# Value products after every step of a 16-dim attention: a kept bank for the sums, three banks in rotation for the scores

## The chip, the cores and the metric

The kernel runs on one core of a Trainium2 chip. A core has TensorE (PE; matrix products, with weight loads on PEld), VectorE (DVE), ScalarE (ACT), GpSimd (POOL) and SyncE (SP), which run side by side and wait for each other by semaphores. TensorE writes only to PSUM, which here is handed out in banks of 128 partitions by 512 fp32 numbers; eight of them exist. VectorE and ScalarE read the banks. The metric is the device time of one execution in microseconds (us); lower is better.

## The reference

Two transformer layers over 1024 tokens of width 256, in fp32, each with an attention and a mixture of experts. The first layer's attention is a gated sum of two: a main one with 16 heads of 192 dims, and a "pattern" attention with 16 heads of 16 dims. The change concerns the second:

```python
pq = split_heads(hidden_states @ sp_q_w.T)
pk = split_heads(hidden_states @ sp_k_w.T)
pv = split_heads(hidden_states @ sp_v_w.T)
p_scores = jnp.einsum('bhqd,bhkd->bhqk', pq, pk) * PD ** (-0.5)
p_probs = jax.nn.softmax(p_scores.astype(jnp.float32), axis=-1).astype(dt)
p_ctx = jnp.einsum('bhqk,bhkd->bhqd', p_probs, pv)
pattern_out = p_ctx.transpose(0, 2, 1, 3).reshape(b, s, HID) @ sp_o_w.T
```

All 1024 keys are seen by every query (no mask). The second layer's attention has 16 heads of 16 dims too, with a causal mask and a bias per head; it runs through the same functions with `causal=True`.

## The kernel before

**Banks.** PSUM is one pool. Two tiles named `sc` take two banks each (`sc_tile`, L52). The other four banks are single: two named `nn` and two named `mm`. `mm_tile` (L55) hands them out in turn, nn, mm, nn, mm, so that a bank comes back after four tiles; a tile that is handed out waits until the last reader of the tile before it in that bank is done.

**The 16-dim attention** (`small_attention`, L253). Four heads form a group; each head sits in 32 of the 128 partitions, so that four score products with 32 rows each run side by side in the four row groups of the array. A unit is one half of the queries (512) and one group of heads: eight units. The work has two sides:

- First scores (`first_pair`, L286): queries on the partitions, 512 keys along the free dimension, two heads into one `sc` tile (L299). VectorE takes the maximum per query (L305, `mx`). When all maxima of a unit are there, `find_maximum` and `put_maximum` turn them over on TensorE (L319, a single bank) and VectorE adds them to the queries (L323, `q2`), so that the second scores come out with the maximum taken off.
- Second scores (`second_pair`, L326): keys on the partitions, 512 queries along the free dimension (L337). ScalarE takes the exponential out of PSUM into `pt`, of one head from a single bank (L347), or, where a step is `wide`, of two heads from an `sc` tile (L344).

A step is one unit and one block of 128 keys: 8 x 8 = 64 steps. As long as first scores of later units are left (steps 0 to 52), a step puts two of them (L299, one `sc` tile each) beside its four second scores: `together(first_pair(*now[0], pair), second(1 - pair))` for two values of `pair`, so two groups of four products. From step 53 on no first scores are left; then odd steps are wide, and even steps put their four second scores into four single banks.

**Value products** (`over_v`, L360). `pt` is multiplied with the values of its key block (L369), four heads into four column groups of one bank `av`. Every second step, in step i with i odd, the products of steps i-3 and i-2 are added up in one single bank from the rotation, eight products in a block. Then ScalarE copies the bank into `cu` where the steps are the unit's first (L375), or VectorE adds it to `cu` (L377). Two steps after the unit's last sum, `divided` (L380) turns `cu` over on TensorE (L385, a single bank), and VectorE divides by the sums of the exponentials.

**Order.** In this stage the order on TensorE is the order in which the program writes it (`tc.manual_schedule` for PE); the other engines' instructions are put in order by the scheduling layer. The stage is driven by the loop of `n_steps` steps with a few products of other work beside steps 38, 39, 53, 55, 57 and 59 (`beside`): the output product of the first half and parts of the main attention's first keys and queries (L655, L668). After it come the main attention's scores (`score_products`, L701, L708).

**Elsewhere** `mm_tile` serves every other product of one bank: projections, transposes, the main attention's four sums (L957), the experts. In the last experts the pool is split: `singles[:] = ["mm", "mm"]`, and the two sums of `modulated_experts` hold the two `nn` banks, then the two `mm` banks.

Of the kernel before, what the change touches and what calls it, by code (L numbers as in the profile page):

```python
# [8 lines left out]
F32 = mybir.dt.float32  # L9
# [5 lines left out]
P = 128  # L15
# [27 lines left out]
def adaln_two_layers(ctx: ExitStack, tc: tile.TileContext, a: dict, out: bass.AP):  # L43
# [5 lines left out]
    psum = ctx.enter_context(pool("psum", 2, space=bass.MemoryType.PSUM))  # L49


    sc_tile = lambda: psum.tile([P, T], F32, tag="sc", name="sc")  # L52
    singles = ["nn", "mm"]

    def mm_tile(tag=None):  # L55
        if tag is None:
            tag = singles[0]
            singles.reverse()
        return psum.tile([P, 512], F32, tag=tag, name=tag)

    turn = [0]

# [114 lines left out]
    def whole(parts):  # L177
        for _ in parts:
            pass
# [73 lines left out]
    def small_attention(sp, qT, kT, v, causal, late):  # L253
# [103 lines left out]
            for it in pairs:  # L357
                next(it, None)

        def over_v(some):  # L360

            u, kc0 = steps[some[0]][:2]
            half, g = units[u]
            av = mm_tile()
            for n in some:
                _, kc, _, q0, _ = steps[n]
                pt = probs.pop(n)
                for j in range(4):
                    nc.tensor.matmul(  # L369
                        av[PW * j : PW * (j + 1), q0:], v[:, kc, 4 * g + j, :], pt[:, j, q0:],  # L370
                        start=(n == some[0]), stop=(n == some[-1]),
                    )
            if kc0 == 0:
                state[u]["cu"] = late[0].tile([P, 512], F32, name="cu", bufs=2)
                nc.scalar.copy(state[u]["cu"], av)  # L375
            else:
                nc.vector.tensor_add(state[u]["cu"], state[u]["cu"], av)  # L377
            return u if steps[some[-1]][2] else None
# [16 lines left out]
        steps = []  # L395
# [26 lines left out]
        ends = []  # L422

        def step(i):
            if i < len(steps):
                u, kc, last, q0, nkc = steps[i]
                probs[i] = late[0].tile([P, 4, 512], F32, name="pt", bufs=6)
                now = [it for _, it in zip(range(counts[i]), beside)]
                for it in now[1:]:
                    first(*it)  # L430


                wide = not now and (causal or i % 2 == 1)
                second = lambda pair: second_pair(u, kc, pair, probs[i], q0, wide)
                if now:
                    for pair in range(2):
                        together(first_pair(*now[0], pair), second(1 - pair))
                else:
                    together(second(0), second(1))
            if i % 4 == 3 and causal and ends:  # L440
                divided(ends.pop())
            go = 4 if causal else 2
            if i % go == 1 and i > go:
                ended = over_v(range(i - go - 1, i - 1))
                if ends:
                    divided(ends.pop())
                if ended is not None:
                    ends.append(ended)
            if i % 4 == 1:
                if i < len(steps) and kc == nkc - 3 and u + 1 < len(units):  # L450
                    find_maximum(u + 1)
                    put_maximum(u + 1)
# [34 lines left out]
    with pool("l0a") as l0, pool("mla") as ml:  # L487
# [228 lines left out]
        with pool("pat") as pat:  # L716
# [142 lines left out]
            with pool("pat2") as pat2:  # L859
                nrm = pat2.tile([P, 4, NH, 16], F32, name="nrm")  # L860

                nrms = [nrm, acc[1].rearrange("p t (h d) -> p t h d", d=16)]
                late += [pat2, nrms]
                mp[0] = pat2

                def put(i, t, ps):
                    nc.vector.tensor_scalar_mul(acc[i][:, t, :], ps, gsm[:, 4 * i + t, 1:2])

                output = small_output(
                    in_two(acc[1].rearrange("p (k i) d -> p k (i d)", k=2)), nrm, sp_o, put, 0
                )
                beside = {
                    38: [lambda: next(output)],
                    39: [lambda: whole(output)],
                    53: [lambda: whole(key_part(0, 0, True))],
                    55: [lambda: whole(query_part(0, 0, True, True))],
                    57: [lambda: whole(key_part(0, 1, True))],
                    59: [lambda: whole(query_part(0, 0, False, True))],  # L880
                }
                with tc.manual_schedule(engines={mybir.EngineType.PE}):
                    for n in range(n_steps):
                        step(n)
                        for fn in beside.get(n, []):
                            fn()
                    score_products(0)
                    last_divided()
                    score_products(1)

        with pool("mla1") as m1, pool("mla2", 2) as m2:
            mp[0] = m2
# [10 lines left out]
            prs, sums, pts, cxs, bcs, rws, avs = {}, {}, {}, {}, {}, {}, {}  # L903
# [93 lines left out]
            for u, (p, i) in enumerate(units):  # L997
                n = 8 * u
# [299 lines left out]
        gate_rows[i] = gD  # L1298
        yield

    def modulated_experts(i, tag, bank):


        sums = [mm_tile(tag) for _ in range(2)]
        chunks = {}

        def hidden(c):
            w = load(a["moe_w"][c].rearrange("p (b m) -> p b m", b=2))
            w1 = w[:, 0, :].rearrange("p (k m) -> p k m", k=2)
            if c % 2 == 0:  # L1310
                chunks["he"] = he_tile()
            ps, he = bank[0](), chunks["he"][:, c % 2, :]
            for k in range(2):
                nc.tensor.matmul(ps, w1[:, k, :], hT[i][:, k, :], start=(k == 0), stop=(k == 1))  # L1314
            nc.scalar.activation(he, ps, AF.Relu, bias=b1[:, c : c + 1])  # L1315
            rows = [(n, r0, r1) for n, r0, r1 in OWNED if r0 < (c + 1) * P and r1 > c * P]
            if len(rows) > 1 or rows[0][0] != NE1:
                g = row_tile()
                for n, r0, r1 in rows:
                    p0, p1 = max(r0 - c * P, 0), min(r1 - c * P, P)  # L1320
                    by = gate_rows[i][n, :].partition_broadcast(p1 - p0) if n is not None else gate_rows[i][:NE1, :]
                    nc.sync.dma_start(g[p0:p1, :], by)
                nc.vector.tensor_mul(he, he, g)  # L1323
            chunks[c] = (he, w[:, 1, :])

        def down(c, b):
            he, w2 = chunks[c]
            for t in (2 * b, 2 * b + 1):

                nc.tensor.matmul(  # L1330
                    sums[b][:, t % 2 * HID : (t % 2 + 1) * HID], he[:, t * P : (t + 1) * P], w2,
                    start=(c == 0 and t % 2 == 0), stop=(c == NC1 - 1 and t % 2 == 1),
                )

        for c in range(NC1):
            hidden(c)
            yield
            if c > 1:
                for b in range(2):
                    down(c - 2, b)  # L1340
                del chunks[c - 2]
                yield

        ov = out.rearrange("o (t p) d -> p (o t) d", p=P)
        for b in range(2):
            for c in (NC1 - 2, NC1 - 1):
                down(c, b)
            yield
            for t in (2 * b, 2 * b + 1):
                at = tmp.tile([P, HID], F32, name="at")  # L1350
                nc.vector.tensor_mul(at, sums[b][:, t % 2 * HID : (t % 2 + 1) * HID], gates_bc[1][:, HID:])
                nc.vector.tensor_add(x[i][:, t, :], x[i][:, t, :], at)
            nc.sync.dma_start(ov[:, 4 * i + 2 * b : 4 * i + 2 * b + 2, :], x[i][:, 2 * b : 2 * b + 2, :])
# [24 lines left out]
    with tc.manual_schedule(engines={mybir.EngineType.PE}):  # L1378
# [49 lines left out]
        bank, half = [mm_tile], [None]  # L1428

        def beside_experts(n):  # L1430
            step(n)
            do(n)
            if n == 37:
                singles[:] = ["mm", "mm"]
                half[0] = modulated_experts(0, "nn", bank)
            if n >= 38:
                next(half[0])

# [6 lines left out]
    with tc.manual_schedule(engines={mybir.EngineType.PE}):  # L1445
        last_divided()
        bank[0] = lambda: sc_tile()[:, :512]
        output = small_output(in_two(he_tile()), nrm, wo, put, 1, bv, (ones, bo))
        inputs = experts_input(1, nc.vector)
        do = side({  # L1450
            1: [(output, 1)], 3: [(output, 2), (inputs, 5)], 9: [(inputs, 1)], 11: [(inputs, 6)], 18: [(inputs, 2)],
        })
        for n, _ in enumerate(half[0]):
            do(n)
        whole(modulated_experts(1, "mm", bank))

# [125 lines left out]
```

## Time and profile before

| quantity | us |
|---|---|
| median of three runs | 1316.52 |
| lowest and highest of them | 1314.94, 1316.79 |
| span of the profiled execution | 1313.1 |
| TensorE busy | 1279.2 |
| VectorE busy | 831.3 |
| ScalarE busy | 625.2 |
| first scores, L299 in this stage, from and to | 75.8 to 256.2 |
| value products of this stage, L369, from and to | 85.3 to 295.3 |

The page gives no time of the profiled execution but its span; the three runs lie 1.8 to 3.7 us above that span. A line of the timeline reads: start, length (us), engine, source line, operation, output <- inputs, shapes, how often (like instructions that overlap or follow each other are merged), and in brackets how long the engine stood before it and what ended the wait. An fp32 product shows as two passes on TensorE, so one product counts as two MATMUL records. A line of the table of stretches reads: the stretch, its length, and for each engine busy us (and instructions), then the granted TensorE clock, the DMA share and GB/s. The granted clock is 1.00 in all stretches.

### The profile page before, as it was taken

Reading aid. Unit: us, or ns where it says so; the run is one execution under the profiler, and the core shown is the slowest. Engines: PE = TensorE matmul, PEld = TensorE weight load, DVE = VectorE, ACT = ScalarE, POOL = GpSimd, SP = SyncE. Lnnn points to the kernel's source line nnn. Section 1 sums busy time; section 2 is a strip of 40 time slices with the busy share of each in tenths; the row PEclk is TensorE's granted clock in tenths of the full one; section 3 lists DMA queues with packets and bytes.
Section 4 is the critical chain, followed back from the end, with each engine's and each line's share of the span. In section 5 each row is a group of like instructions: output and inputs, shape, how many; then the busy total and the mean of one; then the engine's idle time right before and its main releaser. Section 6 shows DMA issues by size and latency. Waiting matters only on the chain.

```text
span 1313.1 us, 25185 instructions
## 1 busy us (share of the span) xinstructions
PE 1279.2 (97%) x10588; PEld 691.4 (53%) x10588; DVE 831.3 (63%) x1282; ACT 625.2 (48%) x1161; POOL 244.3 (19%) x241
## 2 busy tenths in 40 slices
PE   9999999999999999999999999999989999999998
PEld 6532233334555555555555566655656554566665
DVE  4678887737787787888778875344556675252222
ACT  5366665665756657575665433121055565312121
POOL 5000000042535345253533010000000040020000
PEclk9999999999999999999999999999999999999999
DMA  9200000000000000000005022222210000435441
GB/s 281 57 0 1 1 1 1 1 1 17 10 5 6 6 5 6 6 9 2 2 1 162 2 58 70 80 79 70 69 44 10 1 2 9 107 94 164 147 151 56
DMA packets 56666, 58.82 MB, mean 45 GB/s; under 512 B 15143, under 2 KB 42280, under 8 KB 56554
## 3 DMA queue, kind: packets, MB, share of 16 engines
q1 hardware_dynamic: 56010, 57.22, 14.8%
q8 instruction: 83, 1.36, 0.5%
q14 instruction: 29, 0.24, 0.1%
q10 hardware_dynamic: 544, 0.00, 0.0%
HBM read 55.05 MB, written 1.12 MB: 43 GB/s over the span
## 4 chain that ended last, share of the span: by engine, by line
PE 90%; DVE 7%; issue 1%; ACT 1%; DMA 0%; POOL 0%; DVEq 0%; ACTq 0%; POOLq 0%
PE sc L708 16%; PE sc L299 11%; PE mm L957 6%; PE sc L1314 6%; DVE mx L305 4%; PE sc L1198 4%; PE nn L369 4%; PE mm L369 3%; PE nn L1330 3%; PE nn L957 3%; PE mm L1330 3%; PE nn L1176 2%; PE nn L1198 2%; PE mm L1176 2%; PE mm L1198 2%; PE nn L668 2%
## 5 line engine op out<-in xcount | busy, mean ns | idle before, releaser
L305 DVE TENSOR_REDUCE mx<-sc 128x2 f32<-128x1024 f32 (+3 forms) x224 | 239.6, 1106 | 58.2 <-PE sc L299 15.6
L299 PE MATMUL sc<-kT,qT 32*128 32x512 f32 (+3 forms) x896 | 205.0, 584 | 18.4 <-DVE mx L305 18.0
L916 ACT ACTIVATE pr<-sc,nmax 128x1024 f32<-128x1024 f32 x128 | 142.5, 1113 | 166.1 <-DVE nmax L712 160.2
L337 PE MATMUL nn<-q,kT 32*128 32x512 f32 (+3 forms) x384 | 188.0, 589 | 0.0
L337 PE MATMUL mm<-q,kT 32*128 32x512 f32 (+3 forms) x384 | 186.8, 592 | 0.5 <-DVE qf L673 0.5
L925 DVE STREAM_TRANSPOSE pt<-pr 128x1024 f32<-128x1024 f32 x128 | 157.2, 1236 | 40.9 <-ACT pr L916 40.7
L712 DVE TENSOR_REDUCE nmax<-sc 128x1 f32<-128x1024 f32 x128 | 154.2, 1215 | 42.1 <-PE sc L708 40.2
L347 ACT ACTIVATE pt<-nn 128x512 f32<-128x512 f32 (+1 forms) x192 | 106.9, 557 | 59.4 <-PE mm L337 42.8
L347 ACT ACTIVATE pt<-mm 128x512 f32<-128x512 f32 (+1 forms) x192 | 106.9, 557 | 53.7 <-PE nn L337 22.6
L708 PE MATMUL sc<-kf,qf 128*128 128x512 f32 x256 | 120.7, 604 | 2.2 <-ACT pr L916 2.0
L708 PE MATMUL sc<-x,qf 128*128 128x512 f32 x256 | 121.0, 604 | 1.2 <-ACT pr L916 1.1
L957 PE MATMUL mm<-pt,kv 32*64 32x256 f32 x2048 | 122.0, 378 | 0.0
L957 PE MATMUL nn<-pt,kv 32*64 32x256 f32 x2048 | 120.2, 378 | 0.7 <-ACT bc L944 0.7
L299 PEld LDWEIGHTS sc<-kT,qT 32*128 32x128 f32 x896 | 66.3, 183 | 102.0 <-DVE mx L305 86.6
L1323 DVE TENSOR_TENSOR he<-he,row 128x512 f32<-128x512 f32 x46 | 31.7, 692 | 128.9 <-ACT he L1315 100.9
L637 POOL TENSOR_TENSOR t<-t,cos 128x512 f32<-128x512 f32 x32 | 40.7, 1272 | 348.6 <-PE sc L337 217.4
L957 PEld LDWEIGHTS mm<-pt,kv 32*64 32x64 f32 x2048 | 83.5, 131 | 21.9 <-issue 6.2
L957 PEld LDWEIGHTS nn<-pt,kv 32*64 32x64 f32 x2048 | 86.7, 131 | 15.1 <-DVE acc L980 5.3
L1315 ACT ACTIVATE he<-sc,b 128x512 f32<-128x512 f32 x43 | 29.5, 687 | 123.3 <-PE sc L1314 123.3
L1314 PE MATMUL sc<-hT,w 128*128 128x512 f32 x172 | 80.7, 593 | 0.0
L708 PEld LDWEIGHTS sc<-kf,qf 128*128 128x128 f32 x256 | 45.6, 189 | 57.8 <-issue 54.1
L708 PEld LDWEIGHTS sc<-x,qf 128*128 128x128 f32 x256 | 45.6, 190 | 57.7 <-issue 51.4
(378 smaller groups left out, 2116.5 us busy)
## 6 DMA issues: line engine op xcount, KB each, us to landing
w<-in_moe_w_dram SPq DMA_DIRECT2D x50, 256.0 KB
w<-in_wg_dram SPq DMA_DIRECT2D x16, 256.0 KB
w<-in_wu_dram SPq DMA_DIRECT2D x16, 256.0 KB
w<-in_wd_dram SPq DMA_DIRECT2D x16, 256.0 KB
row<-gD SPq DMA_DIRECT2D x14, 256.0 KB
x<-in_x_dram SPq DMA_DIRECT2D x4, 512.0 KB
wo<-in_o_dram SPq DMA_DIRECT2D x1, 2048.0 KB
wm<-in_wmod_dram SPq DMA_DIRECT2D x6, 256.0 KB
```

What stands on the lines that cost most here:

```text
L299: nc.tensor.matmul(sc[:, i, :n], qT[r, g, qt * P : (qt + 1) * P], kT[r, g, c * 512 : c * 512 + n], start=True, stop=not diag,)
L305: nc.vector.tensor_reduce(mx[:, qi, c, 2 * pair : 2 * pair + 2], sc[:, :, :n], AX.X, ALU.max)
L337: nc.tensor.matmul(ps[:, q0:], kT[r, g, kc * P : (kc + 1) * P], state[u]["q2"][r, q0:], start=True, stop=not diag,)
L347: nc.scalar.activation(pt[:, 2 * pair + i, q0:], ps[:, q0:], AF.Exp)
L369: nc.tensor.matmul(av[PW * j : PW * (j + 1), q0:], v[:, kc, 4 * g + j, :], pt[:, j, q0:], start=(n == some[0]), stop=(n == some[-1]),)
L708: nc.tensor.matmul(sc[:, c], qfs[p, i][j][:, t * P : (t + 1) * P], kf[p % 2][j][:, c], start=True, stop=True)
L712: nc.vector.tensor_reduce(nmax, sc, AX.X, ALU.max, negate=True)
L916: nc.scalar.activation(pr, sc, AF.Exp, bias=nmax, accum_out=sums[u][:, t, j : j + 1])
L925: nc.vector.transpose(pts[u][:, :, slice(1, 3) if j else slice(0, 4, 3), 32 * t : 32 * t + 32], prs.pop(n).rearrange("p (b c k) -> p b c k ...
L957: nc.tensor.matmul(av[r][64 * c : 64 * c + 64, : 2 * P], kv32[row, b + c, :], pt[row, b // 2, 2 * c : 2 * c + 2, :].rearrange("p j q -> p ...
L1198: nc.tensor.matmul(gu[s], w[s][:, k, f * P : (f + 1) * P], hT[i][:, k, :], start=(k == 0), stop=(k == 1),)
L1314: nc.tensor.matmul(ps, w1[:, k, :], hT[i][:, k, :], start=(k == 0), stop=(k == 1))
```

## The change

`over_v` is called after every step instead of every second one in the first layer's attention. In step i it multiplies the four heads of step i-2 alone. The products of an even and the following odd step are added up in the same bank: the even one opens the sum (`begin`), the odd one closes it (`end`), and then `cu` is written as before. This bank is now a name of its own, `av`, with one buffer; `mm` is down to one buffer. During the steps `mm_tile` hands out nn, mm, nn in turn, three banks; before and after, nn, mm, nn, av, four. The second layer's attention keeps blocks of four steps and takes its sum from the rotation. The two experts' sums hold `nn, nn` and then `mm, av`.

```diff
-    singles = ["nn", "mm"]
+    banks = {"nn": 2, "mm": 1, "av": 1}
+    singles = ["nn", "mm", "nn", "av"]
 
     def mm_tile(tag=None):
         if tag is None:
-            tag = singles[0]
-            singles.reverse()
-        return psum.tile([P, 512], F32, tag=tag, name=tag)
+            tag = singles.pop(0)
+            singles.append(tag)
+        return psum.tile([P, 512], F32, tag=tag, name=tag, bufs=banks[tag])
...
-        def over_v(some):
+        held = [None]
+        def over_v(some, begin=True, end=True):
 
-            u, kc0 = steps[some[0]][:2]
+            u, kc0 = steps[some[-1] if end and not begin else some[0]][:2]
             half, g = units[u]
-            av = mm_tile()
+            if not causal and begin:
+                held[0] = mm_tile("av")
+            av = mm_tile() if causal else held[0]
             for n in some:
...
-                        start=(n == some[0]), stop=(n == some[-1]),
+                        start=(begin and n == some[0]), stop=(end and n == some[-1]),
                     )
-            if kc0 == 0:
+            if not end:
+                return None
+            if kc0 < 2:
...
-            go = 4 if causal else 2
-            if i % go == 1 and i > go:
-                ended = over_v(range(i - go - 1, i - 1))
+            if not causal and i > 1:
+                ended = over_v([i - 2], i % 2 == 0, i % 2 == 1)
+                if i % 2 and ends:
+                    divided(ends.pop())
+                if ended is not None:
+                    ends.append(ended)
+            if causal and i % 4 == 1 and i > 4:
+                ended = over_v(range(i - 5, i - 1))
                 if ends:
                     divided(ends.pop())
...
                 with tc.manual_schedule(engines={mybir.EngineType.PE}):
+                    singles[:] = ["nn", "mm", "nn"]
                     for n in range(n_steps):
...
                     score_products(1)
+                    singles[:] = ["nn", "mm", "nn", "av"]
...
-    def modulated_experts(i, tag, bank):
+    def modulated_experts(i, tags, bank):
...
-        sums = [mm_tile(tag) for _ in range(2)]
+        sums = [mm_tile(tag) for tag in tags]
...
-                singles[:] = ["mm", "mm"]
-                half[0] = modulated_experts(0, "nn", bank)
+                singles[:] = ["mm", "av"]
+                half[0] = modulated_experts(0, ("nn", "nn"), bank)
...
-        whole(modulated_experts(1, "mm", bank))
+        whole(modulated_experts(1, ("mm", "av"), bank))
```

## The prediction

> **What bounds the kernel now.** I read the page first: its span, its busy table and its chain.
>
> ```profile
> span 1313.1 us, 25185 instructions
> ...
> PE 1279.2 (97%) x10588; PEld 691.4 (53%) x10588; DVE 831.3 (63%) x1282; ACT 625.2 (48%) x1161; POOL 244.3 (19%) x241
> ...
> PE 90%; DVE 7%; issue 1%; ACT 1%; DMA 0%; POOL 0%; DVEq 0%; ACTq 0%; POOLq 0%
> ```
>
> TensorE carries 90% of the chain, so what TensorE is late in this stage the end is late too; nothing later waits for anything else long enough to swallow it. The change touches one stretch, so the numbers must come from there. The table of stretches shows one period (two steps) and, below it, the tail in which no first scores are left:
>
> ```profile
> 126.17:132.68 6.51, 6.05 (x52) 1.85 (x48) 5.40 (x6) 4.23 (x9) 0.00 (x0) 1.00 0.00 0
> 257.20:295.81 38.61, 38.09 (x225) 11.97 (x225) 15.45 (x27) 22.95 (x35) 15.11 (x12) 1.00 0.00 1
> ```
>
> The columns are the stretch, its length, then busy us of PE, PEld, DVE, ACT and POOL. In 6.51 us VectorE works 5.40 and ScalarE 4.23: neither is full. What sets 6.51 is seen in the timeline of one period. A "quad" below is four score products in the four row groups of the array: two first scores (L299) and two second scores (L337).
>
> ```profile
> 128.03 0.70 PE L299 MATMUL sc<-kT,qT 32*128 32x512 f32 x2
> ...
> 129.00 0.59 PE L299 MATMUL sc<-kT,qT 32*128 32x512 f32 x2
> ...
> 129.20 4.81 DVE L305 TENSOR_REDUCE mx<-sc 128x2 f32<-128x1024 f32 x4 [0.35 <-PE nn L337]
> ...
> 130.48 0.70 PE L299 MATMUL sc<-kT,qT 32*128 32x512 f32 x2 [0.46 <-DVE mx L305]
> ...
> 131.02 0.59 PE L299 MATMUL sc<-kT,qT 32*128 32x512 f32 x2
> ...
> 131.61 0.70 PE L299 MATMUL sc<-kT,qT 32*128 32x512 f32 x2
> 131.70 0.60 ACT L347 ACTIVATE pt<-mm 128x512 f32<-128x512 f32 x1 [0.39 <-PE nn L337]
> ...
> 132.15 0.59 PE L299 MATMUL sc<-kT,qT 32*128 32x512 f32 x2
> 132.68 1.92 PE L369 MATMUL mm<-pt,v 128*32 128x512 f32 x16
> ...
> 134.54 0.70 PE L299 MATMUL sc<-kT,qT 32*128 32x512 f32 x2
> 134.68 0.69 DVE L377 TENSOR_TENSOR cu<-cu,mm 128x512 f32<-128x512 f32 x1 [0.66 <-PE mm L369]
> ```
>
> The period is a loop: quad 1 at 128.03, its maxima on VectorE from 129.20, whose end frees the double bank for quad 3 at 130.48 (TensorE idle 0.46), quad 4 at 131.61, the eight value products at 132.68, the next quad 1 at 134.54. A product is two passes: first pass to second 0.54 from standing (130.48 to 131.02), 0.43 in a stream. The 0.66 that VectorE waits before L377 is wait for the value block. The last view is the tail, where one step shows what a late bank does:
>
> ```profile
> 289.37 0.69 PE L337 MATMUL mm<-q,kT 32*128 32x512 f32 x1
> ...
> 289.58 0.69 DVE L377 TENSOR_TENSOR cu<-cu,nn 128x512 f32<-128x512 f32 x1 [4.09 <-PE nn L369]
> ...
> 290.32 0.69 PE L337 MATMUL nn<-q,kT 32*128 32x512 f32 x1
> 290.53 0.60 ACT L347 ACTIVATE pt<-mm 128x512 f32<-128x512 f32 x1 [1.33 <-PE mm L337]
> ```
>
> Three score products start at 289.37; the fourth stands until the bank that held the value sums has been read (289.58 + 0.69 = 290.27) and starts 0.05 later, alone.
>
> **The change, part by part.**
>
> *Value products after every step.* The instruction count is unchanged. VectorE and ScalarE keep their order exactly; on TensorE 31 blocks of four value products move forward past the two quads of the next step. POOL and SP are as before, no DMA moves. A block of eight costs 132.68 to 134.54 = 1.86; with pass sets 0.43 apart (weight loads at 133.14 and 133.57) a block of four, half the sets, costs 1.86 - 2 x 0.43 = 1.00. Two of them cost 2.00, so the split costs 0.14 a period. The Trainium skill says why, in "TensorEngine Tiling (Array Packing)", Key Properties: a change of tiling mode drains TensorE. The trace agrees: quad to value block takes 0.53 (132.15 to 132.68) where a pass in the same mode follows after 0.43, and the rule gives no price of its own; it speaks against the change, and by it alone the sum would be a loss of 26 x 0.14 = 3.6 us. If nothing else were added, this part would be a gain: VectorE's 0.66 goes, and a step would be 0.97 (128.03 to 129.00) + 0.43 + 0.53 + 1.00 = 2.93 instead of 6.51 / 2 = 3.255.
>
> *One bank kept for the sums, three in rotation for the scores.* This is the dear part. Each quad takes two single banks. With four in rotation a bank comes back two quads later. With three it comes back after three tiles: the second L337 product of every quad writes the bank of the first L337 product of the quad just before it, and must wait until ScalarE has taken the exponential out of it. TensorE issues in order, so behind that waiting product stand the step's value products, and behind them the next step's quads, whose maxima and exponentials wait in turn. Between steps the value block covers this (quad B to next quad A is longer than the exponential). Within a step nothing covers it. The chain of a step, from the start of quad A:
> - quad A, first pass to second 0.54, second pass 0.59 (131.02 to 131.61);
> - to the exponential 0.09 (131.61 to 131.70), the exponential 0.60, release 0.05 (290.27 to 290.32): quad B's last product starts at 1.87;
> - alone, 0.54 to its second pass and 0.53 to the value block (132.15 to 132.68): 2.94;
> - value block 1.00, next quad A at 3.94.
>
> The double banks are not late in this loop: the maxima of quad A end at about 1.18 + 1.22, long before 3.94. So a step costs 3.94 - 3.255 = 0.685 more. It applies to steps 2 to 52, the steps that have first scores beside them and value products behind them: 51 x 0.685 = 35 us, against 80.69 to 257.20 in the trace before. Steps 0 and 1 have no value block and are paced by the maxima (2.45 a step, 78.24 to 80.69); there quad B's late product is caught up by the wait that VectorE imposes anyway: 0.
>
> Bounds for the step: if ScalarE's pitch (0.49, the next exponentials at 129.74 and 130.22) and a streaming second pass (0.43) count, 3.94 - 0.11 - 0.11 = 3.72, a loss of 24 us; if each exponential is a further 0.16 late (a copy of the sums at L375, 0.58, ahead of it in one step of four), 4.10, 43 us. I take 3.94, since every term is the row of the same operation.
>
> *The tail, steps 54 to 62.* A narrow step puts four second scores into single banks. Before, the fourth was 0.95 late (289.37 to 290.32) and the wide step ran beside it; narrow, wide and value block took 263.55 to 268.16 = 4.61. After, the fourth waits for the first's exponential: 1.87 + 0.54 + 0.53 = 2.94, value block 1.00, wide quad 0.54 + 0.53 = 1.07, value block 1.00: 6.01, that is 1.4 more for each of four pairs, and 0.6 for the pair at 283.99, which was late already (5.38). Together 6 us; bounds 3 (half hidden by the key parts' banks) and 9.
>
> *Bank names elsewhere.* Outside the stage four banks still turn in a ring of four, and the experts' sums take the same two pairs: 0. If a rename made one wait differ it would be of the size of one eviction, below 1 us.
>
> Sum: 35 + 6 = 41 us. The profiled execution spans 1313.1; the median of the three runs, 1316.52, lies 3.4 above it, a margin that I keep. 1316.5 + 41 = 1357.5; I say 1357.
>
> **The rivals.**
> - *The three banks don't bind, and the split is pure gain.* For it: ScalarE is busy only 4.23 of 6.51, VectorE's 0.66 wait goes. The step is then 2.93: (3.255 - 2.93) x 51 = 17 us, about 1300. It needs the bank to be back when quad B reaches it. The point from which it decides: a step is the release plus 2.07 (0.54 + 0.53 + 1.00), so it beats 3.255 only if the release comes before 1.19 after the start of quad A, and quad A's products themselves end at 1.13. Only a reuse distance of four tiles could do that.
> - *The wait is hidden in TensorE's present idle time.* TensorE already stands 0.46 in a period. If the lone product lay in that time, the kernel would stay at 1316. Against it: the 0.46 is before quad 3, in the middle of what is now one of two equal steps, and the new wait is 0.9 in each step. A half-hidden case would give 1325 to 1340.
> - *ScalarE falls late as well.* The two exponentials of quad B end near 3.7, just before quad A of the next step needs them; the tiles of L319 and L385 enter the same ring of three, and their readers on VectorE gate a score product after them. If each of these 14 tiles costs 0.5 and each exponential queue 0.2 a step, 7 + 10 more: 1375.
> - *The clock falls because TensorE idles more.* The granted clock was 1.00 in all stretches, the tail included; a step's longest stand would be below 1 us. I give it no weight of its own.
>
> **How the numbers follow.** The chain as computed, with its bounds (24 + 3 to 43 + 9, so 1344 to 1368): 0.85. ScalarE late too, 1375: 0.05. Half hidden, 1325 to 1340: 0.03. Hidden, 1316: 0.02. Pure gain, 1300: 0.05. The range is the bounds of the first case, 1344 to 1368; it leaves out 0.15. Within 0.2% (2.6 us) is about what a measurement can tell from no change: slower 0.93, same 0.02, faster 0.05.
>
> **What would show it.** In the timeline after: steps of about 3.9 us; in each step the second L338 product of quad B alone some 0.9 us after the other three, released by the exponential (L348); blocks of four value products (eight passes) about 1.0 us long; no wait before VectorE's addition to cu, but waits of over 1 us before its maxima. VectorE's and ScalarE's busy sums stay. The stretch to the first score of the next part (295.81 before) grows by some 41 us, and after it everything keeps its length. I am wrong if quad B's four products start together, or if the steps are near 3.0 or 3.3 us.

## The result and the profile after

The changed kernel takes 1359.91 us (median of five, 1358.38 to 1361.53) against 1316.53 us for the kernel before beside it (1314.94 to 1318.36): 1.033 times as long, interval 1.0316 to 1.0341. Slower, and 2.9 us above the forecast of 1357.

The profiled execution is the longest of the five. Its page:

```profile
span 1359.8 us, 25184 instructions
...
PE 1335.1 (98%) x10588; PEld 706.0 (52%) x10588; DVE 830.7 (61%) x1282; ACT 629.2 (46%) x1161; POOL 244.6 (18%) x241
...
PEclk9999999997999999999999999999999999999999
...
PE 93%; DVE 4%; ACT 1%; issue 1%; DMA 0%; POOL 0%; DVEq 0%; ACTq 0%; POOLq 0%
```

VectorE and ScalarE do what they did (831.3 and 625.2 us before). TensorE executes as many products and is called busy for 55.9 us more: a moment in which only one row group of the array works counts as busy too, and the late product is such a moment. So the busy share says little here; the starts of the products do. In the line PEclk one slice is no longer 9; the text comes back to it.

Three points of the trace divide the span: the first value block, the wide step 53 and the main attention's first score.

| profiled execution (us) | before | after | longer by |
|---|---|---|---|
| first value block starts | 85.35 | 84.34 | |
| step 53 starts | 257.20 | 292.78 | 35.6, the steps |
| first main score starts | 295.81 | 342.47 | 11.1 more, the tail |
| end of the span | 1313.1 | 1359.8 | 0.0 more, the rest |

One step of the timeline after, of the 3.91 us that a plain step takes (6.51 for two before; in this file L299, L337 and L347 have become L300, L338 and L348, the value products are L374 and VectorE's addition L384). Quad A is the first group of four score products in the step, quad B the second:

```profile
134.06 0.70 PE L300 MATMUL sc<-kT,qT 32*128 32x512 f32 x2
...
135.02 0.59 PE L338 MATMUL nn<-q,kT 32*128 32x512 f32 x1
135.03 0.59 PE L300 MATMUL sc<-kT,qT 32*128 32x512 f32 x2
...
135.23 2.35 DVE L306 TENSOR_REDUCE mx<-sc 128x2 f32<-128x1024 f32 x2 [1.56 <-PE mm L338]
135.27 0.60 ACT L348 ACTIVATE pt<-nn 128x512 f32<-128x512 f32 x1 [1.51 <-PE mm L338]
...
135.92 1.12 PE L338 MATMUL nn<-q,kT 32*128 32x512 f32 x2
...
136.97 1.07 PE L374 MATMUL av<-pt,v 128*32 128x512 f32 x8
...
137.97 0.70 PE L300 MATMUL sc<-kT,qT 32*128 32x512 f32 x2
...
138.11 0.69 DVE L384 TENSOR_TENSOR cu<-cu,av 128x512 f32<-128x512 f32 x1 [0.52 <-PE av L374]
```

Quad A starts at 134.06. The first of its two second scores is taken out by the exponential at 135.27, done at 135.87, and 0.05 later, at 135.92, the last product of quad B gets that bank and runs alone: two passes in one record, 1.12. The value block of four products can't pass it and starts at 136.97, the next step at 137.97. VectorE and ScalarE each stand over 1.5 us of this step (in the next one, with its addition, VectorE works 3.04 of 3.91). A step whose unit turns its maxima or its sums over takes 4.50.

### The profile page after: what moved, and what is told of

Read it like the earlier page. It is cut to its first block, busy times and chain, and to the rows that moved or that the text cites. A ratio compares the mean times of both kernels' runs of the same rounds, so it can differ in the third digit from the quotient of the medians.

```text
span 1359.8 us, 25184 instructions
## 1 busy us (share of the span) xinstructions
PE 1335.1 (98%) x10588; PEld 706.0 (52%) x10588; DVE 830.7 (61%) x1282; ACT 629.2 (46%) x1161; POOL 244.6 (18%) x241
## 3 DMA queue, kind: packets, MB, share of 16 engines
HBM read 55.05 MB, written 1.12 MB: 41 GB/s over the span
## 4 chain that ended last, share of the span: by engine, by line
PE 93%; DVE 4%; ACT 1%; issue 1%; DMA 0%; POOL 0%; DVEq 0%; ACTq 0%; POOLq 0%
PE sc L720 16%; PE sc L300 9%; PE av L374 6%; PE nn L338 5%; PE sc L1328 5%; PE sc L1212 4%; PE mm L971 4%; PE nn L971 3%; PE nn L1344 3%; PE mm L338 3%; PE nn L1190 2%; PE nn L1212 2%; PE av L971 2%; PE nn L680 2%; PE mm L680 2%; DVE mx L306 2%
## 5 line engine op out<-in xcount | busy, mean ns | idle before, releaser
L338 PE MATMUL nn<-q,kT 32*128 32x512 f32 (+1 forms) x462 | 206.9, 599 | 0.7 <-ACT pt L348 0.7
L300 PE MATMUL sc<-kT,qT 32*128 32x512 f32 (+3 forms) x896 | 199.3, 578 | 8.0 <-DVE mx L306 7.6
L348 ACT ACTIVATE pt<-nn 128x512 f32<-128x512 f32 (+1 forms) x231 | 125.7, 562 | 81.9 <-PE nn L338 38.4
L338 PE MATMUL mm<-q,kT 32*128 32x512 f32 (+2 forms) x230 | 119.7, 600 | 0.5 <-DVE qf L685 0.5
L971 PE MATMUL mm<-pt,kv 32*64 32x256 f32 x1024 | 118.5, 378 | 0.0
L971 PE MATMUL av<-pt,kv 32*64 32x256 f32 x1024 | 117.6, 377 | 0.0
L300 PEld LDWEIGHTS sc<-kT,qT 32*128 32x128 f32 x896 | 68.8, 183 | 74.4 <-DVE mx L306 49.8
L348 ACT ACTIVATE pt<-mm 128x512 f32<-128x512 f32 (+2 forms) x115 | 64.7, 562 | 53.7 <-PE nn L338 32.7
L338 PEld LDWEIGHTS nn<-q,kT 32*128 32x128 f32 x462 | 64.5, 183 | 44.2 <-ACT pt L348 26.0
L1329 ACT ACTIVATE he<-sc,b 128x512 f32<-128x512 f32 x43 | 29.6, 687 | 123.3 <-PE sc L1328 123.3
L374 PE MATMUL av<-pt,v 128*32 128x512 f32 (+3 forms) x672 | 85.4, 599 | 0.8 <-DVE cu L384 0.8
```

Source lines behind the costliest of these rows:

```text
L300: nc.tensor.matmul(sc[:, i, :n], qT[r, g, qt * P : (qt + 1) * P], kT[r, g, c * 512 : c * 512 + n], start=True, stop=not diag,)
L338: nc.tensor.matmul(ps[:, q0:], kT[r, g, kc * P : (kc + 1) * P], state[u]["q2"][r, q0:], start=True, stop=not diag,)
L348: nc.scalar.activation(pt[:, 2 * pair + i, q0:], ps[:, q0:], AF.Exp)
L374: nc.tensor.matmul(av[PW * j : PW * (j + 1), q0:], v[:, kc, 4 * g + j, :], pt[:, j, q0:], start=(begin and n == some[0]), stop=(end and n ...
L971: nc.tensor.matmul(av[r][64 * c : 64 * c + 64, : 2 * P], kv32[row, b + c, :], pt[row, b // 2, 2 * c : 2 * c + 2, :].rearrange("p j q -> p ...
```

## The experiments

The theory: the rotation of three single banks costs the time, since a tile's bank comes back after three tiles and each step puts four into it; the exponential then stands in TensorE's way in each step. The rivals: the finer value blocks themselves (twice as many changes between score and value products), the kept bank with its readers, or the slower clock. The trace after settles the last two for the steps: the sum's bank is read out at 138.11 + 0.69 = 138.80 and is next written at 140.89, so nothing waits for it, and the granted clock is 1.00 from 84.34 to 292.78.

**The split without the three banks.** The kernel before, its value products after every step; each step's sum takes a bank of its own from the ring of four and goes to `cu` at once, so there are twice as many additions.

```diff
-            go = 4 if causal else 2
-            if i % go == 1 and i > go:
-                ended = over_v(range(i - go - 1, i - 1))
+            if not causal and i > 1:
+                ended = over_v([i - 2])
+                if i % 2 and ends:
+                    divided(ends.pop())
+                if ended is not None:
+                    ends.append(ended)
+            if causal and i % 4 == 1 and i > 4:
+                ended = over_v(range(i - 5, i - 1))
```

> Only the split: value products after every step, but each step's four in a bank of its own from the ring of four, and VectorE (ScalarE for a unit's first) takes each sum out, so cu is added to twice as often. Theory: a score product waits for an exponential two quads back, which is never late; steps of 2.9 us, and 3.3 where VectorE is still at maxima when the sums should be taken out: mean 3.1 against 3.255, about 1310. Rival (mode changes and blocks are the cost): as many blocks as in the change, so slower than before by most of the 43 us, above 1340.

Measured 1313.14 us against 1317.56 for the kernel before, ratio 0.997 (0.9959 to 0.9982): a little faster. In its timeline quad A, its four products at once in quad B, and the value block follow each other without a stand:

```profile
135.60 0.70 PE L299 MATMUL sc<-kT,qT 32*128 32x512 f32 x2
...
136.13 0.59 PE L299 MATMUL sc<-kT,qT 32*128 32x512 f32 x2
...
136.57 0.59 PE L299 MATMUL sc<-kT,qT 32*128 32x512 f32 x2
136.77 2.36 DVE L305 TENSOR_REDUCE mx<-sc 128x2 f32<-128x1024 f32 x2 [0.84 <-PE nn L337]
...
136.99 0.59 PE L337 MATMUL mm<-q,kT 32*128 32x512 f32 x1
137.00 0.59 PE L337 MATMUL nn<-q,kT 32*128 32x512 f32 x1
...
137.53 1.06 PE L369 MATMUL mm<-pt,v 128*32 128x512 f32 x8
```

135.60 to 137.53 is 1.93 where the step after takes 2.91 (134.06 to 136.97). Step 53 starts at 251.60, 5.6 us earlier than in the kernel before. So with four banks the split is no loss; the rival that blames it alone falls.

**The three banks without the split.** The changed kernel, the value products of two steps in one block again.

```diff
-                ended = over_v([i - 2], i % 2 == 0, i % 2 == 1)
+                ended = over_v([i - 3, i - 2]) if i % 2 and i > 2 else None
```

> Only the three banks: the sums keep their own bank and the scores turn in three, but the value products stay in blocks of eight after every second step. Theory (the second score product of a quad waits for the exponential of the quad before it, because the bank comes back after three tiles): the wait is paid once or twice in a period of two steps, but VectorE's pacing hides a part of it between the two steps; period about 7.2 instead of 6.51 us, about 18 us in the steps and 4 in the tail: about 1340. Rival (the more frequent change of tiling mode and the value blocks themselves are the cost): no more blocks than before, so about 1316.

Measured 1347.11 us, ratio 1.0229 (1.0214 to 1.0244): 29.6 of the 43.4 us, about two thirds of the loss, with the old value blocks. Step 53 starts at 282.72, 25.5 us later than before, where the whole change is 35.6 later; the tail takes 43.5 in place of 38.6, at a clock of 1.00. The period is 7.48, more than the 7.2 expected. Its score products and value block, from the timeline:

```profile
135.41 0.70 PE L300 MATMUL sc<-kT,qT 32*128 32x512 f32 x2
...
137.12 1.08 ACT L348 ACTIVATE pt<-nn 128x512 f32<-128x512 f32 x2
137.28 1.12 PE L338 MATMUL mm<-q,kT 32*128 32x512 f32 x2
...
138.25 0.69 PE L338 MATMUL nn<-q,kT 32*128 32x512 f32 x1
...
139.98 1.12 PE L338 MATMUL nn<-q,kT 32*128 32x512 f32 x2
...
141.03 1.92 PE L374 MATMUL av<-pt,v 128*32 128x512 f32 x16
...
142.89 0.70 PE L300 MATMUL sc<-kT,qT 32*128 32x512 f32 x2
```

Three second scores are late in two steps (137.28, 138.25, 139.98), not two. The one at 138.25 belongs to the quad A of the second step, which no value block precedes: the exponentials that start at 137.12 end at 138.20, and it starts 0.05 later. That is what the prediction said the value block covers. The changed kernel has a value block there, so only one product a step is late, but it pays for twice as many blocks: 3.91 a step against 7.48 / 2 = 3.74. With three banks the split therefore costs another 0.17 a step, and step 53 comes 10.1 us later (292.78 against 282.72); with four banks it was a gain. Some seven tenths of the loss in the steps are the three banks alone, the rest is the split on top of them.

**A longer exponential, with three banks and with four.** If the exponential is on TensorE's path, making it longer must show in full; where it is not, it must show little. In the changed kernel and in the split with four banks, the first exponential of quad A's two tiles is taken twice into the same place, with the same numbers.

```diff
             for i, ps in enumerate(tiles):
-                nc.scalar.activation(pt[:, 2 * pair + i, q0:], ps[:, q0:], AF.Exp)
+                for _ in range(2 if not causal and pair == 1 and i == 0 else 1):
+                    nc.scalar.activation(pt[:, 2 * pair + i, q0:], ps[:, q0:], AF.Exp)
```

> The changed kernel, and in every narrow pair that stands beside quad A the first exponential is taken twice (the same numbers again), so that its bank comes free one ScalarE pitch (0.49 us) later. Theory (each step waits for this exponential): steps of 3.91 + 0.49 = 4.40 us, 51 x 0.49 = 25 us more than the changed kernel: about 1385. Rival (blocks and mode changes set the step, or ScalarE's load is not on the path): ScalarE has more than 1 us of idle time in each step, so 1360.

With three banks: 1391.36 us in one run, 31 us above the changed kernel.

```profile
133.60 0.70 PE L300 MATMUL sc<-kT,qT 32*128 32x512 f32 x2
...
134.81 1.23 ACT L349 ACTIVATE pt<-nn 128x512 f32<-128x512 f32 x2 [1.51 <-PE mm L338]
...
136.09 1.12 PE L338 MATMUL nn<-q,kT 32*128 32x512 f32 x2 [0.50 <-ACT pt L349]
137.15 1.07 PE L375 MATMUL av<-pt,v 128*32 128x512 f32 x8
```

The second exponential starts 0.63 after the first, not the 0.49 expected: the two take 1.23 (134.81 to 136.04) in place of 0.60, the lone product starts 0.05 after them, and the step becomes 4.54 in place of 3.91: the 0.63 arrives one for one, and 51 x 0.63 = 32. The exponential is on the path of every step.

> The same second exponential in the kernel with value products after every step and four banks in the ring. Theory: a bank comes back two quads later, after the exponential even if it is taken twice, so the steps stay near 3.1 us and the time within 5 us of 1313. Rival (an extra exponential costs wherever it stands): 25 us more, 1338.

With four banks: 1328.65 us in one run, 15.5 us above the split alone. This was wrong in its size, and the trace shows why:

```profile
132.94 1.23 ACT L348 ACTIVATE pt<-nn 128x512 f32<-128x512 f32 x2 [0.80 <-PE mm L337]
...
134.22 1.06 PE L370 MATMUL nn<-pt,v 128*32 128x512 f32 x8 [0.49 <-ACT pt L348]
```

The sum of a step is a fifth tile in the ring of four, so the value block takes the bank of the same step's first exponential. With the single exponential that bank is read out 0.12 before the value block (136.81 + 0.60 = 137.41 against 137.53 in the split with four banks); with the double one the block stands 0.49 for it, and a step is 3.49. Score products no longer wait, but four banks are not slack either: the cover is about 0.1 us.

**Part of the change at a time.** First, the changed kernel until step 53, and from step 54 on the ring of four with blocks of eight products:

```diff
+            ring = causal or some[0] >= 52 and len(some) == 2
-            if not causal and begin:
+            if not ring and begin:
                 held[0] = mm_tile("av")
-            av = mm_tile() if causal else held[0]
+            av = mm_tile() if ring else held[0]
...
+            if not causal and i == 54:
+                singles[:] = ["nn", "mm", "nn", "av"]
...
-                ended = over_v([i - 2], i % 2 == 0, i % 2 == 1)
+                if i < 54:
+                    ended = over_v([i - 2], i % 2 == 0, i % 2 == 1)
+                else:
+                    ended = over_v([i - 3, i - 2]) if i % 2 else None
```

> The change up to step 53, and from step 54 the ring of four and blocks of eight as before. Theory: the steps cost 51 x 0.66 = 34 to 36 us and the tail nothing, so about 1352, with the granted clock at 1.00 in the tail. Rival (the tail's cost is a consequence of the late steps, whatever its own order): about 1360, with the clock lowered again.

Measured 1350.07 us, ratio 1.025 (1.0235 to 1.0266). Step 53 starts at 292.75 (292.78 in the changed kernel), and the old tail behind it lasts 36.6 us at full clock, 2.0 less than in the kernel before.

Then the reverse, the kernel before until step 53 and the change from step 54 on (the conditions of the last diff turned round; three banks from step 54):

> The kernel before up to step 53, and the change from step 54 on (three banks, kept bank, blocks of four). Theory: the narrow steps' fourth product waits for the first's exponential; the tail is 6 us longer by the sum of the prediction, up to 11 if the granted clock is halved in some stretches as in the changed kernel: 1323 to 1328. Rival (the tail was long only because the steps ahead of it were late): about 1317.

Measured 1327.19 us, ratio 1.0064 (1.004 to 1.0089), within what was expected. Step 53 starts at 257.08 as before; the tail lasts 48.5 us, 9.8 more than before, of which 3.4 is a stretch of 6.83 us at half speed (290.17 to 297.00); without it the tail is 6.4 longer. Late products are seen here too, and a second thing that no step of the prediction had: the kept bank makes the last value block wait for VectorE's addition.

```profile
303.68 1.93 PE L375 MATMUL av<-pt,v 128*32 128x512 f32 x16 [0.81 <-DVE cu L385]
```

**A version without the loss.** In the split with four banks VectorE's additions, twice as many, stand in front of its maxima. Here ScalarE copies each sum to `ev` and GpSimd adds it to `cu`; `pt` has five buffers in place of six.

```diff
+            elif causal:
                 nc.vector.tensor_add(state[u]["cu"], state[u]["cu"], av)
+            else:
+                ev = late[0].tile([P, 512], F32, name="ev", bufs=2)
+                nc.scalar.copy(ev, av)
+                nc.gpsimd.tensor_add(state[u]["cu"], state[u]["cu"], ev)
```

> Value products after every step, four banks in the ring, and VectorE spared: ScalarE copies every step's sums to SBUF and GpSimd adds them to cu (five buffers for the exponentials instead of six, for room). Theory: neither the ring nor VectorE holds a step, which is then 0.97 + 0.43 + 0.53 + 1.00 = 2.93 us; 51 x 0.325 = 17 us less than before, about 1300. Rival (blocks cost as such): slower than before. If GpSimd's additions slow VectorE or come late for the division: between 1300 and 1316.

Measured 1308.97 us, ratio 0.9934 (0.9917 to 0.9952): faster than the kernel before, but 9 us short. The steps are as expected: a plain step takes 2.93, step 53 starts at 242.71, 14.5 us earlier than before.

```profile
139.31 0.70 PE L299 MATMUL sc<-kT,qT 32*128 32x512 f32 x2
...
139.50 0.58 ACT L380 COPY ev<-mm 128x512 f32<-128x512 f32 x1
...
140.23 1.27 POOL L381 TENSOR_TENSOR cu<-cu,ev 128x512 f32<-128x512 f32 x1 [2.33 <-ACT ev L380]
...
141.24 1.06 PE L369 MATMUL nn<-pt,v 128*32 128x512 f32 x8
```

What is missing lies elsewhere: the tail takes 40.9 where it took 38.6, and the rest 1023.6 where it took 1017.3, at a mean granted clock of 0.996 over the run. Most of what the rest lost is the clock: it runs at half speed in three windows of 3.41 us (from 289.24, 746.63 and 971.90), which is 5.1 of the 6.3 us. In the tail GpSimd now adds sums where it and VectorE turn the main attention's queries by their angles:

```profile
262.03 2.69 POOL L650 TENSOR_TENSOR qf<-t,sw 64x512 f32<-64x512 f32 x2
262.53 5.29 DVE L643 COPY sw<-t 32x512 f32<-32x512 f32 x4
...
264.80 2.74 POOL L381 TENSOR_TENSOR cu<-cu,ev 128x512 f32<-128x512 f32 x2
```

So the last version keeps the copy and GpSimd's addition until step 53, and blocks of eight with VectorE's addition in the tail.

```diff
-            elif causal:
+            elif causal or len(some) == 2:
                 nc.vector.tensor_add(state[u]["cu"], state[u]["cu"], av)
...
-                ended = over_v([i - 2])
+                if i < 54:
+                    ended = over_v([i - 2])
+                else:
+                    ended = over_v([i - 3, i - 2]) if i % 2 else None
```

> As copy_out up to step 53 (blocks of four in the ring of four, ScalarE copies the sums out, GpSimd adds), and blocks of eight with VectorE's addition from step 54 on. Theory: copy_out's tail was 40.9 us long against 38.6 before because GpSimd's additions stand beside VectorE's copies and because of two more blocks a pair; without them it is 37 to 39, so 2 to 4 us less than copy_out: about 1306. Rival: no difference, 1309.

Measured 1300.71 us, ratio 0.9869 (0.9848 to 0.9889), 15.7 us faster than the kernel before (1316.46) and 59 us faster than the changed one. Its tail is 37.2, its rest 1019.1. It was expected at 1306; of its 8.3 us over the version before it, 3.7 lie in the tail, and the profiles put 4.5 into the rest, where nothing was edited. There it has one half-speed window (from 962.94) where the version before it has three, so 3.4 of the 4.5 is the clock and no merit of the edit.

## Why the prediction was right, and where it was off

*The value products after every step, alone (2.93 a step, a split costing 0.14 a period).* Right. The prediction gave this as what the part would be worth if nothing else were added, and 2.93 is what the steps take once nothing else is in the way (139.31 to the start of the value block at 141.24 is 1.93, and 1.00 for the block). The Trainium skill's rule that a change of tiling mode drains TensorE ("TensorEngine Tiling (Array Packing)", Key Properties) speaks against the split; the runs agree that there is a drain, of 0.53 to 0.54 for a pass where 0.43 is usual, and show that it doesn't decide: with twice the changes the split with four banks is faster.

*One bank kept, three in rotation: the chain of a step, 3.94.* Right, 3.91 measured. Its parts from the trace: first and second pass end at 1.12 (134.59 + 0.59 - 134.06; predicted 1.13), the exponential runs from 1.21 to 1.81, release 0.05, quad B's last product at 1.86 (1.87), value block at 2.91 (2.94), next step at 3.91. The sum over the steps, 35, came out as 35.6, in part by luck: steps 4 to 51 became 32.1 longer (0.67 a step, where 0.685 was predicted), and the first four steps and step 52 together 3.5 longer, where the prediction has 2.1. The one-for-one answer of the doubled exponential shows the mechanism, and the rotation of four in the split shows what removes it. The prediction doesn't say how much of this the three banks make alone; the run with blocks of eight does, 25.5 of the 35.6.

*The tail, +6.* The mechanism was right, the size was not: 11.1 in the profiled execution. The pairs (a narrow step, a wide step and what stands beside them) from the tables of stretches of the two kernels, before and then after; the columns are the stretch, its length, busy us of PE, PEld, DVE, ACT and POOL, then the granted clock:

```profile
263.55:270.27 6.72, 6.72 (x37) 1.99 (x36) 3.05 (x6) 3.90 (x6) 3.78 (x3) 1.00 0.00 0
270.27:276.80 6.53, 6.53 (x37) 2.08 (x36) 3.40 (x6) 3.90 (x6) 4.68 (x4) 1.00 0.00 0
276.80:283.99 7.19, 7.19 (x41) 2.39 (x40) 3.69 (x7) 4.38 (x7) 5.32 (x5) 1.00 0.01 3
283.99:289.37 5.38, 4.87 (x33) 1.43 (x32) 1.38 (x2) 4.00 (x6) 1.34 (x2) 1.00 0.00 0
289.37:295.81 6.44, 6.44 (x53) 1.99 (x49) 1.38 (x2) 3.90 (x6) 0.00 (x0) 1.00 0.00 0
```

```profile
297.15:305.18 8.03, 8.03 (x38) 2.10 (x37) 3.05 (x6) 4.11 (x6) 5.04 (x4) 1.00 0.00 0
305.18:314.65 9.47, 9.47 (x37) 2.42 (x37) 3.05 (x6) 4.11 (x6) 5.04 (x5) 0.82 0.00 0
314.65:323.07 8.42, 8.42 (x41) 2.49 (x40) 3.05 (x7) 4.59 (x7) 5.04 (x4) 1.00 0.01 3
323.07:332.22 9.15, 8.63 (x33) 1.71 (x33) 1.38 (x2) 3.72 (x6) 0.00 (x0) 0.63 0.00 0
332.22:342.47 10.25, 8.76 (x53) 1.89 (x49) 1.37 (x2) 4.50 (x7) 0.00 (x0) 0.83 0.00 0
```

The two pairs at full clock are 1.31 and 1.23 longer; 1.4 was predicted. The other three run at 0.82, 0.63 and 0.83: if they lost just what the clock withheld, that is 9.47 x 0.18 + 9.15 x 0.37 + 10.25 x 0.17 = 6.8 us. Without it the tail's loss is 4.3, inside the bounds of 3 to 9: 1.3 + 1.2 + 1.2 + 0.4 for the pair that was late already (0.6 predicted) + 2.1 for the last one, whose value block waits 0.8 for the addition to `cu`, less 2.0 that the stretch from step 53 to the first narrow step got shorter (6.35 to 4.37), of which the smaller value block explains 0.9 and step 53's wide scores the other 1.1:

```profile
257.20 2.26 PE L337 MATMUL sc<-q,kT 32*128 32x512 f32 x8 [0.39 <-DVE mx L305]
```

```profile
292.78 1.14 PE L338 MATMUL sc<-q,kT 32*128 32x512 f32 x8
```

Before, the second wide tile of step 53 waits for maxima that VectorE ends at 258.28 (it starts at 258.33), and the value block comes 2.19 after 257.20; after, the slower steps let VectorE finish at 292.40, and it comes 1.07 after 292.78. The prediction had neither this gain of 2.0 nor the last block's wait of 0.8. Where the steps ahead are the old ones, in the run with the changed tail alone, the tail is 6.4 longer without the clock: the predicted 6 was the right size for what the tail itself costs, and the two misses in the changed kernel, 2.0 less and 6.8 more by the clock, have opposite signs.

*The rival "the clock falls", dismissed with no weight.* This is the step that failed. It stood on the granted clock of 1.00 in the trace before and on stands below 1 us. The stands are as short as that, and the clock fell all the same, in half-speed windows. A row of the same operation at both clocks, in the tail after:

```profile
300.01 1.06 PE L374 MATMUL av<-pt,v 128*32 128x512 f32 x8
...
308.04 1.91 PE L374 MATMUL av<-pt,v 128*32 128x512 f32 x8
```

The miss was worth some 6.8 us in the profiled execution. The medians differ by 43.4, not 46.7 as the profiled executions do; the steps' 35.6 and a tail of 4.3 leave 3.5 for the clock there, an estimate, since the kernel before isn't always at 1.00 either: over its executions beside the experiments the mean clock lies between 0.995 and 1.000. So the forecast of 1357 is near 1359.91 partly by luck: the tail's unforeseen gain of 2.0 and the clock's loss work against each other. That the tail's part is no accident of one run is shown by the changed tail alone (0.93 over its 48.5 us), by the one behind the doubled exponential with three banks (0.96 over 44.8 us), and by the old tail behind changed steps (36.6, at 1.00).

*Elsewhere 0.* Right: 1017.3 us from the first main score to the end in both kernels.

*What would show it.* The lone product, 0.9 behind the other three (135.02 to 135.92), the blocks of 1.0 and the waits of 1.56 before the maxima are there, these in every second step only: after an addition to `cu` VectorE waits 0.35 for its maxima (139.14). "No wait before VectorE's addition to `cu`" was wrong: it stands 0.52 there (138.11). It is harmless, as VectorE then waits for the quads.

*The rivals.* Pure gain needed a reuse distance of four tiles, as the prediction said; that kernel exists, as the split with four banks. Hidden in TensorE's idle time: refuted by steps of 3.91. ScalarE late too: not seen; quad A's second passes end at 135.20 and the exponential starts at 135.27, and a step that turns over its maxima or sums costs 0.59 more (4.50 against 3.91) as it did before (a period of 7.10 against 6.51).

## What to carry to other kernels

Count the tiles that are in flight between a bank's filling and its last read, not the share of busy time: ScalarE worked 2.17 us of a step of 3.91, and its 0.60 us still set the step, since four tiles went through three banks. To price one bank less, write the chain from first use to reuse with rows of the present trace; that gave 3.94 where 3.91 came. A finer split can gain with one number of banks and lose with one less: here it gained with four and cost 10 us with three. Where one is wanted, look for the accumulator outside PSUM first: copying each sum out and adding it on an idle engine kept the four banks and turned the loss of 43 us into a gain of 16.

## What the runs showed of the hardware

- *The clock halves without a long stand.* The half-speed stretches last 3.4 or 6.8 us. Three stretches of the tail after, at full clock, 0.57 and 0.50:

```profile
300.00:304.00 4.00, 4.00 (x27) 0.92 (x26) 0.69 (x1) 2.36 (x3) 3.85 (x4) 1.00 0.00 0
308.00:312.00 4.00, 4.00 (x21) 0.86 (x24) 0.00 (x0) 0.68 (x2) 3.85 (x4) 0.57 0.00 0
328.00:332.00 4.00, 4.00 (x20) 0.72 (x16) 0.00 (x0) 1.33 (x2) 0.00 (x0) 0.50 0.00 0
```

  TensorE stands no longer than about 0.8 us at a time there. The Trainium skill's page "TensorE: Matmul & The Clock Gate" (section "Why this matters for your kernels") asks for pauses under about 3 us; here that was kept, and half speed came. Of the ten profiled executions, the three with late single products in the tail and blocks of four there have such windows in it; the other seven tails have none. But the changed kernel's steps have late single products and blocks of four too, and run at 1.00. The cause stays open; no run here isolated it.
- *What a window costs.* The same windows come elsewhere: in the run with the old tail at 788 to 792 us (0.63) and 1012 to 1016 us (0.79). The part from the first main score on, the same work in all ten executions, takes 1017.3 us where it has no window before its last microseconds (three executions), 1018.9 to 1019.1 with one window of 3.41 us (four), 1020.7 with two (two) and 1023.6 with three (one). A window costs about 1.7 us, half its length, so differences of a few us between two runs need a look at the clock before they are put down to an edit.
- *Products in different row groups can start out of the program's order.* The program puts the two first scores of a quad ahead of its two second scores. In the run with three banks and blocks of eight, in the quad behind the late product of 137.28 (second pass at 137.81), the first of the first scores starts at 137.86, a second score at 137.88 and the other first score only at 138.24, 0.43 after the late product's second pass.
- *A repeat in place is kept apart by a semaphore.* Two exponentials into different tiles start 0.50 apart (136.81, 137.31 in the split with four banks: the timeline's rows for `mm` and `nn`); into the same place they take 1.23 together, 0.63 apart. There the second one's record names a wait for the semaphore that the first raises, so this is no figure for the engine alone.
- *VectorE stands beside GpSimd.* In the version with the copy, four copies of 32 x 512 on VectorE take 1.71 us in the row below, where GpSimd is idle, and 5.29 (the row at 262.53) where GpSimd works all the time, on four additions one after the other; two of these take 2.74 (264.80) where one alone takes 1.27 (140.23). The Trainium skill tells in "SBUF — State Buffer" (section "SBUF: two separate sides") that some VectorE instructions and GpSimd share a pair of ports of which one holds the whole for an instruction's length; the two rows fit that, with VectorE the one that stands.

```profile
248.50 1.71 DVE L643 COPY sw<-t 32x512 f32<-32x512 f32 x4
```
